# Layer 1's sort in a two-layer graph kernel: sums by even quarters, group ends looked up from two sides, tables of two values, first rows by small transfers

## The chip, the cores and the metric

One core of a Trainium2 chip runs the whole program. The metric is the device time of one execution in microseconds (us), as the median of several runs. The profile is of one further execution of the same program.

## The reference, cut to what matters

Two graph layers follow each other over 2708 nodes with 128 features and a dense 0/1 matrix `adj`. Only the second one is touched by the change:

```python
XW = X @ W                                   # X: output of layer 0
s_col, s_row = XW @ a[0, :f], XW @ a[0, f:]
Z1  = leaky_relu(s_row[:, None] + s_col[None, :], 0.01)
den = exp(Z1)
num = A @ den
att = where(num != 0, den / num, 0)
x   = layernorm(X + A @ (att @ XW))
```

`den[k, j]` depends on the sign of `s_row[k] + s_col[j]` alone in its form: it is `exp(s_row) * exp(s_col)` on one side and the same with 0.01 in the exponents on the other. So the kernel orders the nodes k by `-s_row` and the nodes j by `s_col`, cuts both orders at common thresholds into 24 groups of at most 126 nodes, and keeps running sums: for the nodes j of one group only the 126 rows k of the same group need a mixed treatment, all others are in two sums, carried from group to group in rows 0 and 1 of a 128-row operand.

## The kernel before, in words

**Layer 0** ends with a pass (L696) over six strips of 512 columns of the transposed matrix (`strip0` to `strip5`, the last 148 wide); each strip gives 4 blocks of nodes (the last one 2) their layer 0 output `x1`, and with it `s_row`, `s_col` (tiles `sr_p`, `sc_p`), `x1 @ W` (`xw`, sent to memory) and counts of nodes beyond 256 thresholds (`tally`, into `cnt`). `e2_w` holds `exp(0.01 s_row)` per node, 32 columns wide, as weights.

**Sums over everything** (`tot`, PSUM, two banks) are the start of the carried rows: `e2_w` of each of 22 row blocks times the whole row block of the transposed matrix. Each product uses 32 of TensorE's columns (`tile_position=(0, 32 * q)`), so that products with different q stand side by side. A job `total_early(kb)` ("e") loads columns 0 to 1535 of row block kb into one of three `nat` buffers, by a transfer that POOL issues, and takes them in four pieces of 384 columns, q = 0 to 3. A job `total_kept(kb)` ("k") takes strips 3, 4 and 5, which are still in SBUF, with 512, 512 and 148 columns, q = 0 to 2. Five "e" each are done at strips 3 and 4; the other 12 and all 22 "k" are strewn as fillers (`fill("kekkek...")`) among TensorE's instructions of the sort.

**The sort** starts when `strict` is set at the last strip: from there `pinned` (L163 to L167) ties every instruction of TensorE, VectorE and part of ScalarE's to the one before, so that the order in the program is the order on the engine. That is why nearly all its lines are L167. POOL and SP follow the scheduler's own order. Its steps are:

1. The counts go to all partitions (`ct`, `spread_ps`), and `reached` finds for each of 256 thresholds how far one group starting there can go (`nxt_b`, L654, L780).
2. `ends` (L827 to L834): 23 dependent look-ups in `nxt_b`, one for each group after the first, then `hit`, `thr_ps`, `thr`: the 24 thresholds in use.
3. For k, then j: `beyond` (`k_gt`), `grouped_by` (`k_hot`: node in group; `k_run`: its number there; `ahead`), `placed` (`k_onp`: node at place, in two halves), `valued` (L898: 22 small ScalarE products for each value, `k_ons`), `table` (`tab_ps`, 22 products of 32 columns per value, then `sel`). k has three values, node number, `exp(s_row)` and `exp(0.01 s_row)`; j has two, node number and `s_col`.
4. `gather` (L954): an indirect transfer, issued by POOL, of a group's 126 rows of the transposed matrix into `ring` (4 buffers over the memory of the strips); `gather_xw` (L964) the same of `xw` into `xws`.
5. `carry_in` (L987): `tot` is copied (`carried`), turned to rows 0 and 1 of `ring[0]` by 7 TensorE products (`in_ps`) and 7 copies.
6. The weights of groups 0 to 3: `c_s`, `g_s`, products `gb`, then `weights` (L1050) on ScalarE. Those of groups 4 to 23 go through memory (`g_d`, then a spread to all partitions, L1072).

**The main loop** (L1128) has 24 steps of `num` (6 products), a logarithm, a subtraction, an exponential and, three steps later, 5 products into `m_acc`. **The last part** multiplies once more by the matrix, read again from memory (L1228), and normalizes. Some checks on sizes (L1182 to L1207) feed a branch at the end; the scheduler put several of them into the sort.

Of the kernel before, what the change touches and what calls it, by code (L numbers as in the profile page):

```python
# [15 lines left out]
P = 128  # L16
# [20 lines left out]
PARTS = ((0, 1024), (1024, 2048), (2048, TAIL), (TAIL, N))  # L37
KEPT = 3
# [6 lines left out]
def grouped(  # L45
# [64 lines left out]
    def counted(name, pattern, base, step, size):  # L110
# [23 lines left out]
    row0, row1, rest, head = (  # L134
        const.tile([P, 1], F32, name=n) for n in ("row0", "row1", "rest", "head")
# [4 lines left out]
    def constants():  # L140
        dve("tensor_scalar", pad, node, N - 0.5, 1e6, ALU.is_gt, ALU.mult)
        dve("tensor_scalar", from_n, node, float(-N), None, ALU.add)
        dve("tensor_scalar", after_node, node[:, 0:2], 1.0, None, ALU.add)
        dve("tensor_scalar", row0, node[:, 0:1], 0.0, None, ALU.is_equal)
        dve("tensor_scalar", row1, node[:, 0:1], 1.0, None, ALU.is_equal)
        dve("tensor_scalar", rest, node[:, 0:1], 1.5, None, ALU.is_gt)

        dve("tensor_scalar", head, node[:, 0:1], 1.5, TINY, ALU.is_lt, ALU.max)
        dve("tensor_reduce", four, ident.rearrange("p (q g) -> p g q", q=4), AX.X, ALU.add)
# [33 lines left out]
    def act(op, *args, **kwargs):  # L183
        if strict:
            pinned("ACT", getattr(nc.scalar, op), *args, **kwargs)
        else:
            getattr(nc.scalar, op)(*args, **kwargs)  # L187

# [421 lines left out]

    tot = ps_tot.tile([P, 2, SW], F32, name="tot")
    early = KEPT * SW // 4

    def total_early(kb):
        a = nat.tile([P, KEPT * SW], F32, tag="nat", name="nat")
        nc.gpsimd.dma_start(a, adj_t[ts(kb, P), : KEPT * SW])
        for q in range(4):
            mm(
                nc.tensor.matmul, tot[32 * q : 32 * q + 32, 0, :early], e2_w[:, kb, :],
                a[:, q * early : (q + 1) * early],  # L620
                start=(kb == 0), stop=(kb == NB - 1),
                tile_position=(0, 32 * q), skip_group_check=True,
            )

    def total_kept(kb):
        for q in range(NS - KEPT):
            s = KEPT + q
            mm(
                nc.tensor.matmul, tot[32 * q : 32 * q + 32, 1, : width(s)], e2_w[:, kb, :],
                strips[s][:, kb, : width(s)],  # L630
                start=(kb == 0), stop=(kb == NB - 1),
                tile_position=(0, 32 * q), skip_group_check=True,
            )

# [8 lines left out]

    kept = [(total_kept, kb) for kb in range(NB)]
    others = [(total_early, kb) for kb in range(10, NB)]

    def fill(pattern):

        for c in pattern:
            f, kb = (kept if c == "k" else others).pop(0)  # L650
            f(kb)


    nxt_b = late.tile([P, Q], F32, name="nxt_b")  # L654
# [11 lines left out]
    def reached(ct_ps):  # L666

        nxt = small.tile([P, 2], F32, tag="nxt", name="nxt")
        for h in range(2):
            more = work2.tile([P, SW], F32, tag="junk", name="more")[:, :Q]  # L670
            dve("tensor_scalar", more, ct_ps[:, :Q], ct[:, h : h + 1], None, ALU.subtract)
            dve(
                "scalar_tensor_tensor", more, ct_ps[:, Q:], ct[:, 2 + h : 3 + h], more,
                ALU.subtract, ALU.max,
            )
            fits = work2.tile([P, SW], F32, tag="junk", name="fits")[:, :Q]
            dve(
                "tensor_scalar", fits, more, G + 0.5, 0.0, ALU.is_lt, ALU.add,
                accum_out=nxt[:, h : h + 1],
            )  # L680
        return nxt
# [14 lines left out]
    for s in range(NS):  # L696
# [32 lines left out]
        if strict:  # L729
            fill("ekkk")  # L730
# [6 lines left out]
        )  # L737

# [10 lines left out]
        if strict:  # L749

            dve("tensor_reduce", ct, cnt.rearrange("p s k h -> p (k h) s"), AX.X, ALU.add)
            fill("k")
            ct_ps = spread_out(ct, 4)
            fill("k")
# [11 lines left out]
        nc.scalar.activation(e2_p[:, mine], low[:, mine], AF.Exp, scale=LEAK)  # L766
        nc.gpsimd.tensor_copy(e2_w[:, mine, 1], e2_p[:, mine])
        if strict:
            nxt = reached(ct_ps)
            nxt_ps = spread_out(nxt, 2)  # L770
        pn = ps_mm.tile([P, SW // P, D], F32, tag="mm", name="xw_ps")
# [5 lines left out]
        xw = work2.tile([P, SW // P, D], F32, tag="xw", name="xw")  # L777
        if strict:
            nc.scalar.copy(xw[:, :nb, :], pn[:, :nb, :])
            dve("tensor_copy", nxt_b, nxt_ps[:, :Q])  # L780
# [6 lines left out]
        if s in (3, 4):  # L787
            for kb in range(5 * s - 15, 5 * s - 10):
                total_early(kb)
    fill("kekkekkekkekkk")  # L790
# [20 lines left out]
    e1_p = tab.tile([P, NB], F32, name="e1_p")  # L811
    nc.scalar.activation(e1_p, low, AF.Exp)
# [8 lines left out]
    ons = {"k": (3, None), "j": (2, None)}  # L821
    for name, (m, _) in ons.items():
        t = tmp.tile([P, m, NB, 32], F32, name=name + "_ons")
# [3 lines left out]
    ends = tmp.tile([P, NG], F32, name="ends")  # L827
    dve("tensor_copy", ends[:, 0:1], nxt_b[:, 0:1])
    for g in range(1, NG):
        junk = tmp.tile([P, Q], F32, tag="more", name="junk")  # L830
        dve(
            "scalar_tensor_tensor", junk, bound_no, ends[:, g - 1 : g], nxt_b,
            ALU.is_equal, ALU.mult, accum_out=ends[:, g : g + 1],
        )  # L834
    thr_ps = ps_x.tile([P, SW], F32, tag="x", name="thr_ps", bufs=2)
    for h in range(2):
        hit = tmp.tile([P, NG], F32, tag=f"hit{h}", name="hit")
        dve(
            "tensor_scalar", hit, ends, after_node[:, h : h + 1], theta[:, h : h + 1],
            ALU.is_equal, ALU.mult,  # L840
        )
        mm(
            nc.tensor.matmul, thr_ps[:, :NG], ones, hit, start=(h == 0), stop=(h == 1)
        )
    fill("kkk")
    thr = tmp.tile([P, NG + 1], F32, name="thr")
    nc.gpsimd.memset(thr[:, 0:1], -1e9)
    dve("tensor_copy", thr[:, 1:], thr_ps[:, :NG])


    def beyond(name, v):

        gt = tmp.tile([P, NG + 1, NB], F32, name=name + "_gt")
# [3 lines left out]
    def grouped_by(name, gt):  # L857
# [3 lines left out]
        run = tmp.tile([P, NG, NB], F32, name=name + "_run")  # L861
# [9 lines left out]
        return hot, run, ahead, of  # L871

    def placed(name, hot, run, ahead):

        dve(
            "tensor_tensor", ons[name][:, 0, :, :NG].rearrange("p b g -> p g b"), hot,
            along(from_n, NG, NB), ALU.mult,
        )
        dve("tensor_tensor", run, run, over(ahead[:, :NG], NG, NB), ALU.add)
        own = tmp.tile([P, NB, NG], F32, tag="own", name=name + "_own")  # L880
        dve("tensor_tensor", own.rearrange("p b g -> p g b"), run, hot, ALU.mult)
        at = tmp.tile([P, NB], F32, name=name + "_at")
        dve("tensor_reduce", at, own, AX.X, ALU.add)

        halves = []
        for b0, b1 in ((0, 12), (12, NB)):
            onp = tmp.tile([P, b1 - b0, P], F32, tag=f"onp{b0}", name=f"{name}_onp{b0}")
            dve(
                "tensor_tensor", onp, over(at[:, b0:b1], b1 - b0, P),
                along(col, b1 - b0, P), ALU.is_equal,  # L890
            )
            halves += [onp[:, b, :] for b in range(b1 - b0)]
        return halves

    def valued(name, k, hot, val):

        for b in range(NB):
            nc.scalar.activation(  # L898
                ons[name][:, k, b, :NG], hot[:, :, b], AF.Identity, scale=val[:, b : b + 1]
            )  # L900

    def table(name, onp, values, ps, p0=0, between=""):

        t = tmp.tile([P, len(values), P], F32, name=f"{name}_t{values[0]}")
        for b0 in range(0, NB, 4):
# [8 lines left out]
        for n, o in enumerate(ps):  # L914
            nc.scalar.copy(t[:, n, :], o)
        if callable(between):
            between()
        else:
            fill(between)
# [17 lines left out]

    k_gt = beyond("k", vk)
    k_hot, k_run, k_ahead, k_of = grouped_by("k", k_gt)
    valued("k", 1, k_hot, e1_p)  # L940
    valued("k", 2, k_hot, e2_p)
    fill("ekkekkee")
    j_gt = beyond("j", vj)
    k_onp = placed("k", k_hot, k_run, k_ahead)
    k_tab, _ = table("k", k_onp, [0], banks("x"), P - G)
    j_hot, j_run, j_ahead, j_of = grouped_by("j", j_gt)
    k_no = rows_of_table("k", k_tab, G)
    valued("j", 1, j_hot, sc_p)
    k_tab, _ = table("k", k_onp, [1, 2], banks("x", "ahead"), between="eee")
    assert not kept and not others, (len(kept), len(others))  # L950

# [21 lines left out]
    j_onp = placed("j", j_hot, j_run, j_ahead)  # L973
    carried = tmp.tile([P, 2, SW], F32, name="carried")
    nc.gpsimd.memset(carried, 0.0)
    for r0, r1, k, c in ((0, P, 0, early), (0, 64, 1, SW), (64, 96, 1, width(NS - 1))):
        nc.scalar.copy(carried[r0:r1, k, :c], tot[r0:r1, k, :c])
# [5 lines left out]
    carried_parts = [(q, 0, q * early, early) for q in range(4)] + [  # L983
        (s - KEPT, 1, s * SW, width(s)) for s in range(KEPT, NS)
    ]

    def carry_in(*nos, by, ps=None):  # L987

        for n in nos:
            q, k, i0, c = carried_parts[n]  # L990
            o = (ps or ps_x).tile(
                [P, SW], F32, tag="num" if ps else "sel", name="in_ps", bufs=3 if ps else 2
            )
            mm(
                nc.tensor.matmul, o[:2, :c], ident[:, 32 * q : 32 * q + 2],
# [700 lines left out]
```

## Time and profile before

| | us |
|---|---|
| median of 3 runs (762.22 to 765.44) | 762.48 |
| the profiled execution's own time | 763.92 |
| its span, first to last instruction | 762.0 |
| last strip's first step in the sort (`h`) | 359.2 |
| first look-up of `ends` | 373.06 |
| first `num` of the main loop | 419.12 |
| `num` of steps 8 to 23, start to start | 8.84 |
| first `h_acc` of the last part | 649.33 |

Times in the trace are from the start of the span. A row of the timeline gives start, duration, engine, line, operation, result and operands, how often, and in brackets how long the engine stood idle before it and what ended that. TensorE takes each float32 product in two passes, so x8 in a row is four products. A row of merged instructions spans gaps, and PE rows of the four column groups lie over each other. The table of stretches gives for each engine its busy time and instructions, then the share of the TensorE clock that was granted, the busy share of the DMA engines and their rate.

### The profile page before, as it was taken

What the parts mean: (1) busy time and instruction counts of PE and PEld (TensorE: products, weight loads), DVE (VectorE), ACT (ScalarE), POOL (GpSimd) and SP (SyncE); (2) the same over time, 40 slices, a digit from 0 to 9 for tenths busy, and PEclk for the clock granted to TensorE, in tenths of its full rate; (3) what the DMA queues carried; (4) which work ended last, traced back from release to release, by engine and by line L of the source; (5) the groups of instructions that cost most, each with busy time, mean ns of one, the idle gap of its engine ahead of it and who ended that gap; (6) DMA issues with size and microseconds to landing.
All of it is one profiled execution on the core that took longest, in us unless ns stands there. A gap on an engine that the chain in (4) does not pass through costs nothing. (4 is left out here: it accounts for less than half of the span.)

```text
span 762.0 us, 7796 instructions
## 1 busy us (share of the span) xinstructions
PE 721.7 (95%) x2561; PEld 350.4 (46%) x2561; DVE 453.2 (59%) x947; ACT 419.7 (55%) x601; POOL 259.1 (34%) x255
## 2 busy tenths in 40 slices
PE   6989999999997999999898799999999999999995
PEld 4434454545553444445334344444444445544444
DVE  4786776664631443235895998998999982203032
ACT  4747777868551222112264599999999994001000
POOL 6857696979741000001124887111111000000000
PEclk9999999999998999999999999999999999999999
DMA  8738988898989996535369835964444430898970
GB/s 299 282 134 317 313 321 310 321 342 302 345 305 412 379 346 240 188 125 208 117 243 241 255 102 187 223 187 158 173 171 143 157 135 1 269 314 301 319 236 22
DMA packets 67522, 179.87 MB, mean 236 GB/s; under 512 B 4238, under 2 KB 18354, under 8 KB 64450
## 3 DMA queue, kind: packets, MB, share of 16 engines
q1 hardware_dynamic: 52996, 123.10, 45.7%
q0 software_dynamic: 8208, 53.30, 22.1%
q10 hardware_dynamic: 6270, 2.90, 1.3%
q8 instruction: 22, 0.36, 0.2%
q14 instruction: 26, 0.21, 0.1%
HBM read 176.44 MB, written 2.84 MB: 235 GB/s over the span
## 5 line engine op out<-in xcount | busy, mean ns | idle before, releaser
L541 POOL TENSOR_TENSOR total<-total,p_t 128x512 f32<-128x512 f32 (+2 forms) x132 | 152.4, 1155 | 44.5 <-ACT p_t L187 28.3
L167 PE MATMUL num<-ring,wt 128*128 128x512 f32 (+1 forms) x288 | 128.3, 545 | 7.5 <-DVE q L167 4.9
L167 PE MATMUL m_acc<-q,xws 128*128 128x512 f32 x240 | 120.5, 592 | 0.4 <-ACT q L167 0.4
L703 PE MATMUL dif_acc<-strip,x_sb 128*128 128x512 f32 (+1 forms) x264 | 107.7, 557 | 5.3 <-DVE x_sb L582 4.6
L181 DVE SCALAR_TENSOR_TENSOR p_t<-sim,gentle,piece 128x512 f32<-128x512 f32 (+1 forms) x111 | 71.3, 670 | 50.2 <-PE sim L175 35.9
L175 PE MATMUL att_acc<-p_t,x_sb 128*128 128x512 f32 (+1 forms) x228 | 97.2, 545 | 3.4 <-ACT p_t L187 3.1
L167 DVE COPY q<-num 128x512 f32<-128x512 f32 x144 | 86.4, 613 | 16.6 <-PE num L167 15.5
L1233 PE MATMUL h_acc<-ring,m_sb 128*128 128x512 f32 x220 | 95.7, 593 | 0.0
L187 ACT ACTIVATE p_t<-p_t,shift 128x512 f32<-128x512 f32 (+1 forms) x111 | 69.4, 656 | 31.4 <-DVE p_t L181 30.8
L167 PEld LDWEIGHTS num<-ring,wt 128*128 128x128 f32 x288 | 51.5, 190 | 67.4 <-issue 55.7
L167 DVE SCALAR_TENSOR_TENSOR q<-sr_b,nc_s,q 128x1536 f32<-128x1536 f32 (+1 forms) x48 | 77.4, 1613 | 1.2 <-ACT q L167 1.2
L167 ACT ACTIVATE q<-q,head,rest 128x1536 f32<-128x1536 f32 (+1 forms) x48 | 70.5, 1509 | 8.5 <-DVE ring L167 4.5
L703 PEld LDWEIGHTS dif_acc<-strip,x_sb 128*128 128x128 f32 x264 | 47.2, 194 | 56.0 <-issue 49.5
L167 PEld LDWEIGHTS m_acc<-q,xws 128*128 128x128 f32 x240 | 45.5, 190 | 57.1 <-issue 55.7
L954 POOL DMA_INDIRECT ring<-in_adj_t,k_no x24 | 33.5, 1397 | 108.0 <-PE num L167 103.1
L167 ACT ACTIVATE row<-row 128x1354 f32<-128x1354 f32 x44 | 58.3, 1324 | 17.6 <-DMA row<-in_adj 17.2
L1233 PEld LDWEIGHTS h_acc<-ring,m_sb 128*128 128x128 f32 x220 | 41.3, 190 | 49.3 <-issue 49.3
L167 ACT ACT_TABLE_LOAD x48 | 61.6, 1283 | 3.8 <-issue 2.9
L167 ACT ACTIVATE q<-q,c_s 128x1536 f32<-128x1536 f32 (+1 forms) x48 | 62.7, 1354 | 0.3
L175 PEld LDWEIGHTS att_acc<-p_t,x_sb 128*128 128x128 f32 x228 | 39.1, 190 | 49.6 <-ACT p_t L187 27.6
L1248 DVE TENSOR_TENSOR hh<-rows,x 128x512 f32<-128x512 f32 (+1 forms) x6 | 3.8, 641 | 85.2 <-PE rows L1171 82.5
L1243 ACT COPY ht<-h_acc 128x512 f32<-128x512 f32 (+1 forms) x6 | 3.2, 536 | 91.3 <-PE h_acc L1233 91.2
(270 smaller groups left out, 823.0 us busy)
## 6 DMA issues: line engine op xcount, KB each, us to landing
row<-in_adj SPq DMA_DIRECT2D x44, 677.0 KB, 5.8
strip<-in_adj_t SPq DMA_DIRECT2D x10, 2816.0 KB, 14.8
ring<-in_adj_t SPq DMA_DIRECT2D x27, 1024.0 KB, 5.0
piece<-in_adj_t SPq DMA_DIRECT2D x24, 1024.0 KB, 6.2
nat<-in_adj_t POOLq DMA_DIRECT2D x22, 768.0 KB
piece<-in_adj_t SPq DMA_DIRECT2D x7, 512.0 KB, 6.0
strip<-in_adj_t SPq DMA_DIRECT2D x2, 814.0 KB, 13.8
last<-in_adj_t POOLq DMA_DIRECT2D x1, 1628.0 KB
```

What stands on the lines that cost most here:

```text
L167: latest[engine] = op(*args, **kwargs)
L175: op(*args, **kwargs)
L181: getattr(nc.vector, op)(*args, **kwargs)
L187: getattr(nc.scalar, op)(*args, **kwargs)
L541: nc.gpsimd.tensor_tensor(total[:r, :v], total[:r, :v], p_t[:r, :v], ALU.add)
L703: nc.tensor.matmul(acc[:, :v], x_sb[:, jb, :], st[:, jb, :v], start=(jb == 0), stop=(jb == NB - 1),)
L954: nc.gpsimd.indirect_dma_start(out=ring[g % RING][P - G :, :], out_offset=None, in_=adj_t[:, :], in_offset=bass.IndirectOffsetOnAxis(ap=k_ ...
L1233: nc.tensor.matmul(acc[:, : h1 - h0], m_sb[:, kb + b, :], a[:, b, h0:h1], start=(kb + b == 0), stop=(kb + b == NB - 1),)
L1243: nc.scalar.copy(ht[:, h0:h1], acc[:, : h1 - h0])
L1248: nc.vector.tensor_tensor(hh[:, b0 : b0 + n, :], rows[:, :n, :], x1[:, ib + b0 : ib + b0 + n, :], ALU.add)
```

## The change

- "k" takes the kept columns in four quarters of 293, q = 0 to 3; a quarter that runs over the end of a strip is taken in two pieces, so a job has 6 products instead of 3. Strips 3 and 4 have four "e" each, so 14 stay for the sort; those are loaded by transfers that SP issues. The fill patterns are new.
- At strip 4 no exponential is taken; the last strip's one covers both (`s != NS - 2`).
- `reached` needs two VectorE instructions for each half instead of three. `ends`: partitions 0 to 63 go up from the first threshold, partitions 64 to 127 down from the last one, with 11 look-ups at once. For that the number of fitting thresholds is also summed over partitions by two products of 256 columns (`ones` by `fits`), and one more product (`ends_ps`) brings both sides together.
- k's table has two values, number and `s_row`, and j's number and a clipped `s_col`; the exponentials come after the table, of 24 columns. Node numbers of k are valued by ScalarE, those of j by VectorE. `onp` is made in one instruction.
- `carry_in` is gone: eight transfers of 2 rows, issued by SP, take `carried` to rows 0 and 1 of `ring[0]`.
- The first four groups' weights come from products of `four` by `j_t` between j's table and its `sel`; group 0's exponential and weights go first.
- The checks are tied behind the main loop. The order on POOL has all four first `gather` ahead of the first `gather_xw`; before, three.

The core of the diff:

```diff
-    others = [(total_early, kb) for kb in range(10, NB)]
+    quarters = (KEPT * SW // 4, (N - KEPT * SW) // 4)
+    def first_strips(kb, eng):
+        a = nat.tile([P, KEPT * SW], F32, tag="nat", name="nat")
+        eng.dma_start(a, adj_t[ts(kb, P), : KEPT * SW])
+        for q in range(4):
+            sum_part(0, q, kb, 0, a[:, ts(q, quarters[0])])
+    def kept_strips(kb, eng):
+        for _, q, s, i, c, n in sorted(kept_parts):
+            sum_part(1, q, kb, c, strips[s][:, kb, i : i + n])
...
-            fill("ekkk")
+            fill("kekek")
...
+            for h in range(2):
+                mm(nc.tensor.matmul, nxt_ps[:, Q:], ones, fits[h], start=(h == 0), stop=(h == 1))
...
-    fill("kekkekkekkekkk")
+    fill("kekekkekek")
...
-    for g in range(1, NG):
+    for g in range(1, half_g):
...
+    mm(nc.tensor.matmul, ends_ps[:, : NG - 1], ones, both, start=True, stop=True)
...
-    valued("k", 1, k_hot, e1_p)
-    valued("k", 2, k_hot, e2_p)
-    fill("ekkekkee")
+    valued("k", 0, k_hot, from_n)
+    valued("k", 1, k_hot, low, 0, 18)
+    fill("kekekek")
     j_gt = beyond("j", vj)
...
-    k_tab, _ = table("k", k_onp, [0], banks("x"), P - G)
+    k_tab, _ = table("k", k_onp, [0], banks("x"), P - G, between=lambda: fill("e"))
+    valued("k", 1, k_hot, low, 18)
+    j_run, j_ahead, j_of = numbered("j", j_hot)
+    fill("ke")
+    valued_by_dve("j", 0, j_hot, from_n)
     k_no = rows_of_table("k", k_tab, G)
-    valued("j", 1, j_hot, sc_p)
-    k_tab, _ = table("k", k_onp, [1, 2], banks("x", "ahead"), between="eee")
+    for n, c in enumerate(quarters):
+        act("copy", carried[:, n, :c], tot[:, n, :c])
...
+    for n, c in enumerate(quarters):
+        for q in range(4):
+            i = n * KEPT * SW + q * c
+            nc.sync.dma_start(ring[0][:2, i : i + c], carried[32 * q : 32 * q + 2, n, :c])
     for g in range(2):
         gather(g)
+    j_own = chosen("j", j_hot, j_run, j_ahead)
+    valued("j", 1, j_hot, cs_p)
+    k_tab, _ = table("k", k_onp, [1], banks("x"))
+    j_onp = placed("j", j_own)
...
+    def first_weights():
+        gb_ps = ps_x.tile([P, 4, P], F32, tag="x", name="gb_ps", bufs=2)
+        for g in range(4):
+            mm(nc.tensor.matmul, gb_ps[:, g, :], four[:, g : g + 1].to_broadcast([P, P]), j_t_of[1], ...)
+        act("activation", gb[:, 0, :], gb_ps[:, 0, P - G :], AF.Exp)
+        weights(0, gb[:, 0, :])
+        act("activation", gb[:, 1:, :], gb_ps[:, 1:, P - G :], AF.Exp)
+    j_tab, j_t = table("j", j_onp, [0, 1], banks("x", "ahead"), between=first_weights)
```

## The prediction

> **What bounds the kernel now.** I read the page's busy shares, then the table of stretches, then each engine's timeline over the sort. TensorE is busy 95% of the span, but not everywhere with work that counts:
>
> ```profile
> core 0: us, PE busy (x) PEld busy (x) DVE busy (x) ACT busy (x) POOL busy (x), PEclk, DMA share, GB/s
> ...
> 372.00:387.00 15.00, 14.99 (x110) 5.73 (x111) 13.19 (x55) 0.37 (x1) 4.00 (x8) 0.89 0.64 219
> 387.00:400.00 13.00, 11.18 (x130) 4.92 (x130) 12.72 (x18) 11.89 (x51) 2.18 (x5) 1.00 0.57 193
> 400.00:406.00 6.00, 4.30 (x112) 3.10 (x100) 5.83 (x6) 4.21 (x19) 5.39 (x3) 1.00 0.84 247
> 406.00:419.10 13.10, 11.94 (x128) 6.31 (x121) 3.85 (x14) 4.19 (x12) 3.67 (x5) 0.87 0.96 238
> ...
> 480.00:690.00 210.00, 208.88 (x569) 99.60 (x568) 144.60 (x187) 159.54 (x148) 16.70 (x15) 1.00 0.56 176
> ```
>
> In the main loop (480 to 690) TensorE is the bound. In the sort its busy time is mostly filler. What sets the sort's length changes: VectorE to 400, then TensorE's written order.
>
> ```profile
> L167 DVE SCALAR_TENSOR_TENSOR junk<-bound_no,ends,nxt_b x23: 484/485/486, 373.1 to 384.7; 128x256 f32<-128x256 f32 x23
> ```
>
> The 23 look-ups start 0.53 us apart (373.06, 373.59, 374.12): 373.06 to 385.24.
>
> ```profile
> 388.11 10.44 ACT L898 ACTIVATE k_ons<-k_hot,e_p 128x24 f32<-128x24 f32 x44 [15.02 <-DVE k_hot L167]
> ...
> 405.52 0.85 PE L167 MATMUL tot<-nat,e_w 128*32 128x384 f32 x8 [1.70 <-DMA nat<-in_adj_t]
> 406.30 0.62 PE L167 MATMUL k_sel<-four,k_t 128*128 128x24 f32 x4
> 407.02 2.08 PE L167 MATMUL in_ps<-carried,ident 128*2 128x384 f32 x3
> ...
> 409.54 3.18 PE L167 MATMUL tab_ps<-j_onp,j_ons 128*32 128x128 f32 x82
> 412.56 0.81 PE L167 MATMUL in_ps<-carried,ident 128*2 128x384 f32 x2
> ```
>
> After 402, j's table waits behind the last "e" (a late load), k's `sel` and the carry-in. `num` starts at 419.12, and everything behind it follows.
>
> **The change, step by step.** Times are before -> after in the profile's time.
>
> *Price of the fillers.* The timeline shows an "e" at 379.07 and the next at 381.43: 2.36 us for two "k" and one "e", 2 x 2 x 512 + 2 x 384 = 2816 columns of one column group, 0.838 ns each. So "k" costs 0.86 and "e" 0.64; the new "k" has 293 columns in each group, 2 x 293 x 0.838 = 0.49.
>
> *1. Strips 3 and 4.* Two "e" leave a stretch where PE is busy 50.8 of 51 us (305 to 356). One lies ahead of strip 4's `sb_ps` (354.56), whose VectorE work ends only at 359.2: -0.64.
>
> *2. Last strip.* Strip 4's exponential goes, and with it two table switches (1.28 us each); `rstd` waited for the second (VectorE idle 0.98). `xw_ps` now stands after one "k" and a quarter of an "e", so VectorE's 1.27 idle there stays nearly whole. With 0.64, 0.98 and the stray check (0.14): `x1` turned at 364.26 -> 362.5. Filler before it: 3 x 0.49 + 2 x 0.64 + `xw_ps` 1.16 from 358.0, done by 362.0: no wait.
>
> *3. Counts and `reached`.* Same lengths to `more` (368.73 -> 367.0). Six instructions and three checks took 2.96 us; four take 2 x (0.40 + 0.53) = 1.9, end 368.9. "kek" (1.62) ends at 368.6, so it does not hold the spread. New behind it: two products of 256 columns (4 x 256 x 0.838 = 0.86), then `xw_ps`, ScalarE's `xw` copy (0.37) and, queued behind that, its half of `reach_b` (0.37). Look-ups start 373.06 -> 371.75.
>
> *4. Look-ups.* 12 fewer x 0.53 = -6.36: end 385.24 -> 377.6. "kekekkekek" (5.5 us from 370.6) ends by 377.
>
> *5. New joint.* 385.24 to 386.60 was `hit`, `thr_ps`, `thr`; now two `both` (0.25), `ends_ps` (0.40, as `ahead`), `hit`, `thr_ps`, two `thr`, two `cs_p` (0.20): 2.5. `k_gt` 386.6 -> 380.1.
>
> *6. k's table.* VectorE's `k_ons` (0.95) goes: `k_onp` 394.03 -> 386.5. It is now whole before the first product: 3.05, 389.6. `tab_ps` 22 products (1.4) to 391.0. ScalarE has 22 + 18 values at 10.44 / 44 = 0.237: from 381.55 to 391.0, a tie. `k_t`, one "e" (0.64), `sel`: 398.98 -> 391.75. `k_no` (behind `j_ons` by VectorE, 1.12) 399.44 -> 392.9; `gather` 399.94 -> 393.5.
>
> *7. The last fillers.* "ke" ends at 393.7. ScalarE, in order: four values, then the two `carried` copies wait for it (to 394.8), then 22 `j_ons` (5.3, to 400.1; 403.9 before), then k's second `k_t`. Queued behind that wait are j's values and everything of ScalarE's; TensorE waits at `k_sel` to 400.4, with j's table behind it. VectorE's `j_onp` is ready at 399.1, hidden by 1.3.
>
> *8. j's table.* From 400.8, after `k_sel`. 88 passes at the row's 82 in 3.18, or k's 86 in 2.71 at full clock: 2.8 to 3.4. Here a rule speaks against the change. The row first: 406 to 419.1 had a granted clock of 0.87, 13.1 x 0.13 = 1.7 us lost, with PE busy 91%. The Trainium skill, "TensorE: Matmul & The Clock Gate" (The HAM clock gate), says that TensorE falls to half clock after an idle window of about 3.4 us and needs as long busy to return. The new order leaves it idle from 395.1 to 400.4. By the row alone the table ends at 403.9; by the rule it runs at half clock to about 404, 1.5 more. I take 1.4: 405.2.
>
> *9. To the first `num`.* 14 passes of carry-in go. `j_t` copies (0.48), four `gb` products (0.86 + 0.2), exponential 0.3, weights 0.45: 407.4, against 419.12. Not shown before: whether the exponential waits for all four products (0) or one (-0.5); I take all. That is **-11.7**.
>
> *10. Main loop.* No instruction changes, but one stall may go:
>
> ```profile
> PE num L167 <- DMA ring<-in_adj_t,k_no: 1.5, 1, 1.5
> ```
>
> It is group 6, issued by POOL at 459.91 behind 20 `gather_xw`; now it stands behind 17, and group 5 behind 8 instead of 11: **-1.5**. The first groups land about 6 us apart (227 GB/s in 408 to 418 for 1.37 MB each), the first some 8 us after its issue at 393.5: 401.5, 407.5, 413.5, 419.5, needed at 407.4, 412.6, 419.4, 427.5.
>
> *11. Queues.* SP had nothing in the sort but `g_d`; now 14 loads stand ahead of that, each waiting until the "e" three before it has freed its buffer. The nearest row, `ring` in the page's issues, has 1.02 MB in 5.0 us; an estimate from it for 0.79 MB is 4. So the load issued at 371.7 lands at 375.7, 0.7 after TensorE could take it, inside the 0.9 that "kekekkekek" has to spare, and all later ones land 1 us or more before their "e". At 6 us each the last would come 1.4 late, which is in the second rival. POOL loses 12 such issues (0.53). The four `gather` go ahead of `gather_xw`: `xws` 2 us later, first needed at 440. The tied checks stand after `m_sb`, where VectorE idles: 0; otherwise 0.9 us.
>
> *12. Eight small transfers.* Nearest row:
>
> ```profile
> 416.60 0.39 SPq L1038 DMA_DIRECT2D g_d<-g_r  x1
> 422.74 0.68 SPq L1072 DMA_DIRECT2D wt<-g_d  x1
> ```
>
> The second issue waited for the first to land: 6.1 us at most, under gathers. Issues 8 x 0.39 from 394.8 end at 398; + 6.1 = 404, 3.4 before `num`: cost 0. If they queue for one another, see the rivals.
>
> Sum -13.2: 763.92 -> 750.7. The profiled execution is 1.44 over the median 762.48, so **749.3**.
>
> **Rivals.**
>
> *Given back to transfers, about 754.* `wt` of groups 4 on: `g_d` issued near 408, landed 414, spread 14.7 us, 428.8; wanted 24.7 after `num` starts (443.8 - 419.12), at 432. The slack falls from 6.4 to 3.3, as `g_d` gains less than `num`. Four gathers instead of three run then. 8 us late costs 5: 754. The same if "e" loads need 6 us (+1.5 to 2 at step 7) and group 6 stays late. For: DMA share 0.96 in 406 to 419. Against: POOL's loads no longer share the gathers' queue.
>
> *Slower: the eight small transfers in single file.* Place: `num` of group 0 and SP's queue, with `g_d` behind. The Trainium skill ("DMA: Bandwidth & Descriptors", Why a DMA increments its semaphore by 16 and not by 1) puts a 2-row copy on two engines only, always the same lowest ones; its fixed price there (Anatomy of one DMA) is about 2 us. Eight at 2 us in file would end at 411, +3.4: 752.7. At `g_d`'s 6.1 each they end at 443.6: 786. It decides from (419.1 - 394.8) / 8 = 3.0 us each. Against: nothing in the trace shows the next waiting for the last, and `g_d`'s 24 rows took 6.1 together.
>
> *No change.* The 23 look-ups do become 11 in the instruction order, so it does what it says; only if transfers hold the loop throughout would it show nothing. The loop runs at PE 99% from 480 on, against it.
>
> **How the numbers follow.** The sum: 0.64, with 746.5 to 752 (clock -1.4, exponential -0.5; step 7 and the loop stall +1.5 each). Given back: 0.25, 752 to 758. Within 0.5% (3.8 us, about what a measurement of this kernel can tell from no change): 0.06. Slower: 0.05. Faster in all 0.89. Range 745 to 757, which leaves the last part of the second case and the last two outside.
>
> **What would show it.** Right: look-ups x11; `k_gt` near 380; `k_sel` twice, the second after ScalarE's j values; PE idle about 5 us before j's table and a clock below 1 there; first `num` 406 to 409; no wait of `num` on a ring; SP's small transfers landed before. Wrong: `num` waiting on `carried` transfers, PE's "e" waiting on `nat`, ScalarE waiting for `wt` at step 2, or `num` before 404.

## The result, and the profile after

The changed kernel takes 765.85 us (median of 20 runs); the kernel before, run beside it, 762.43 (20 runs). The ratio is 1.0039, 95% interval 1.0019 to 1.0059: slower by 0.4%, where 749.3 was forecast. The ratios leave out the few executions that took over 1.5% more than the fastest of their kernel.

The profiled execution of the changed kernel has a span of 767.8 us against 762.0. Both are cut here at the same instructions. The first row ends at POOL's third copy into `e2_w`, ahead of all that the change touches but one small constant, and differs all the same, from execution to execution: it lay between 304.2 and 309.7 in the 18 profiles of this study, so one profile can't rank two kernels here.

| us | before | after | difference |
|---|---|---|---|
| start to that copy | 306.30 | 309.69 | +3.39 |
| copy to `num` 0 | 112.82 | 103.58 | -9.24 |
| `num` 0 to `num` 8 | 66.38 | 78.27 | +11.89 |
| `num` 8 to the end of `num` 23 | 141.52 | 141.52 | 0.00 |
| the rest | 134.98 | 134.76 | -0.22 |

The sort is 9.2 shorter in this pair, and the first eight steps of the loop give back 11.9. The 9.2 is the upper end: in the three experiments below whose sort is that of the kernel before, but for POOL's order (e2, e6, e10), copy to `num` 0 took 110.7 each, so 2.1 of it may belong to the one profile before, with its wait of 1.7 for an "e" and half clock behind it. The changed sort took 103.1 to 107.9 in the profiles below that leave it alone. The 11.9 are step 6 (7.1 longer), step 7 (2.3), step 4 (1.9) and step 2 (0.6, which e10 has too).

A time after is called "moved" below when 3.39 is taken off it, so that it can be held against the prediction. The table of stretches of the changed kernel:

```profile
core 0: us, PE busy (x) PEld busy (x) DVE busy (x) ACT busy (x) POOL busy (x), PEclk, DMA share, GB/s
...
400.00:406.00 6.00, 1.13 (x14) 1.05 (x18) 3.55 (x3) 5.09 (x23) 5.12 (x3) 0.74 0.70 242
406.00:413.20 7.20, 6.17 (x98) 5.31 (x90) 0.94 (x7) 1.76 (x7) 1.47 (x2) 0.74 0.97 244
413.20:444.00 30.80, 26.63 (x60) 11.24 (x60) 28.44 (x37) 19.04 (x19) 20.76 (x13) 0.94 0.97 223
444.00:492.00 48.00, 38.33 (x89) 17.01 (x89) 32.69 (x41) 40.27 (x37) 29.11 (x19) 0.93 0.51 144
492.00:690.00 198.00, 196.99 (x535) 94.12 (x534) 138.57 (x185) 150.84 (x139) 16.75 (x15) 1.00 0.50 169
```

In 444 to 492 TensorE is idle for almost 10 us and its clock is below 1, while the DMA engines are busy 51% of the time only. So bytes are not short there; something is issued late. From TensorE's waits and its timeline:

```profile
PE num L169 <- DMA ring<-in_adj_t,k_no: 6.9, 1, 6.9
...
PE k_sel L169 <- ACT k_t L169: 5.0, 1, 5.0
PE tot L169 <- DMA nat<-in_adj_t: 4.0, 5, 1.5
...
ACT wt L169 <- DMA wt<-g_d: 3.7, 1, 3.7
PE num L169 <- ACT tails L169: 2.5, 2, 1.3
```

```profile
404.87 0.62 PE L169 MATMUL k_sel<-four,k_t 128*128 128x24 f32 x2 [4.95 <-ACT k_t L169]
405.42 4.91 PE L169 MATMUL tab_ps<-j_onp,j_ons 128*32 128x128 f32 x88
...
413.27 1.98 PE L169 MATMUL num<-ring,wt 128*128 128x512 f32 x4 [0.72 <-ACT g_r L169]
...
480.44 2.05 PE L169 MATMUL num<-ring,wt 128*128 128x512 f32 x2 [6.91 <-DMA ring<-in_adj_t,k_no]
482.28 1.91 PE L169 MATMUL m_acc<-q,xws 128*128 128x512 f32 x2
```

The 6.9 is the gather of group 7, and the two products behind it take 2 us instead of 1: the clock is at half until 484.8.

```profile
478.00:484.80 6.80, 4.36 (x5) 1.85 (x6) 0.69 (x1) 4.09 (x4) 0.59 (x1) 0.50 1.01 288
```

POOL's timeline (of the changed kernel) shows why that gather is late: it stands behind all 24 `gather_xw`, which can start only when `j_no` is there.

```profile
412.80 1.04 POOL L1008 DMA_INDIRECT xws<-xw_d,j_no  x1 [5.70 <-DVE nc_s L169]
...
422.33 1.50 POOL L1008 DMA_INDIRECT xws<-xw_d,j_no  x1 [1.42 <-DMA ring<-in_adj_t,k_no]
429.29 1.00 POOL L1008 DMA_INDIRECT xws<-xw_d,j_no  x1 [5.46 <-DMA ring<-in_adj_t,k_no]
...
456.27 1.39 POOL L998 DMA_INDIRECT ring<-in_adj_t,k_no  x1 [0.30 <-issue]
...
472.52 1.73 POOL L998 DMA_INDIRECT ring<-in_adj_t,k_no  x1 [0.30 <-PE num L169]
```

The first and the last of these rows in the kernel before:

```profile
414.72 1.04 POOL L964 DMA_INDIRECT xws<-xw_d,j_no  x1 [8.51 <-DVE j_no L167]
...
468.76 1.08 POOL L954 DMA_INDIRECT ring<-in_adj_t,k_no  x1 [0.30 <-issue]
```

From the first `gather_xw` to group 7's gather POOL needed 54.0 us before and 59.7 after. It used to arrive just in time: step 7 followed its issue by 7.9 in both kernels, without a wait before. Now TensorE wants it sooner and gets it later.

Group 6, the row at 456.27, is late as well. Step 5 takes 10.61, as it took 10.55 before with its wait of 1.5 for that gather. Step 6's `num` started at 464.45, 8.2 after the issue (7.8 before). The row of this 1.3 names ScalarE's `tails`, which `num` doesn't read, so I take the wait to be the gather's. Step 4 is 1.9 longer (8.84 to 10.69): ScalarE waited 3.7 for `wt<-g_d`.

### The profile page after: what moved, and what is told of

Its sections match the earlier page's. It is cut to its first block, busy times and chain, and to the rows that moved or that the text cites. A ratio compares the mean times of both kernels' runs of the same rounds, so it can differ in the third digit from the quotient of the medians.

```text
span 767.8 us, 7942 instructions
## 1 busy us (share of the span) xinstructions
PE 714.3 (93%) x2639; PEld 357.8 (47%) x2639; DVE 444.8 (58%) x920; ACT 415.4 (54%) x596; POOL 251.0 (33%) x240
## 5 line engine op out<-in xcount | busy, mean ns | idle before, releaser
L169 PE MATMUL num<-ring,wt 128*128 128x512 f32 (+1 forms) x288 | 131.7, 556 | 13.3 <-DMA ring<-in_adj_t,k_no 6.9
```

The source lines that it names most:

```text
L169: latest[engine] = op(*args, **kwargs)
```

## The experiments

The theory at first (1): POOL's chain sets group 7's gather, so an earlier `num` 0 can't be used. Rivals: the DMA engines are simply full (2); the late `wt` and half clock are the main part (3); the sort isn't shorter at all (4). Each ratio is to the kernel before on the same chip; steps and stretches are of one profile each.

**e1, POOL's order written out**, and **e2, the same for the kernel before.** `pinned("POOL", ...)` ties the transfers (the core of the edit):

```diff
-        nc.gpsimd.indirect_dma_start(
+        pinned("POOL", nc.gpsimd.indirect_dma_start,
...
-        gather_xw(g)
     for g in range(2, RING):
         gather(g)
+    for g in range(4):
+        gather_xw(g)
```

So POOL's order is four gathers, four `gather_xw`, then at each step one of each.

> The changed kernel with POOL's transfers in an order written out: four gathers, four gather_xw, then at each step one gather and one gather_xw. Theory 1 (group 7's gather is late because POOL starts it only behind all 24 gather_xw, counted from j_no): num no longer waits for a ring, steps 6 and 7 fall from 15.99 and 11.10 us to about 8.9, so 9 us less than the changed kernel: ratio to before about 0.991 (755 to 757 us). Rival 2 (the gathers themselves land late because the DMA engines are full with four of them): the wait only moves to another group, within 2 us of the changed kernel, ratio 1.00. Rival 3 (late wt and half clock are the main part): step 4 stays at 10.7, at most 2 us are won.

Measured: 1.0080 [1.0052, 1.0109]. Steps 5 to 8 are 8.83 each, the ring's wait is gone, and yet nothing is won: steps 3 and 4 take 14.62 and 13.86.

```profile
ACT wt L169 <- DMA wt<-g_d: 9.8, 1, 9.8
...
PE num L169 <- ACT wt L169: 5.3, 1, 5.3
```

> The kernel before with the same written order of POOL's transfers as in the first run. Theory 1: before had a wait of only 1.5 us for group 6 and its group 7 was issued 8 us early, so it gains about 1.5 us: ratio 0.998. If this order were worth the same to both kernels (the change is not what makes it matter), it gains 8 us or more: 0.99.

Measured: 1.0047 [1.0020, 1.0073], a loss as well; `num` 0 to `num` 8 is 70.2, with steps 3 and 4 at 10.63 and 12.37. So theory 1 was half right: the ring's wait was POOL's order, but with four gathers first ScalarE waited for `wt` in both kernels (9.8 and 5.8). Rival 3 lives.

**e3, POOL's order of the kernel before in the changed one.**

> The changed kernel with POOL's transfers in exactly the order of the kernel before (3 gathers, 4 gather_xw, 1 gather, 3, 1, 4, 1, 9, 1, 4, 1). Theory 1, in the form that the chain of 24 gather_xw from j_no is the limit whatever its order: group 7 is issued 54 us after j_no (412.8) at about 467 instead of 472.5, so the stall falls from 6.9 to about 1.5 to 2: ratio about 0.997. If the order had nothing to do with it (rival 2), the same as the changed kernel, 1.004.

Measured: 1.0016 [0.9995, 1.0037]. With three gathers first, steps 0 to 4 have no stall (5.26, 6.76, 8.75, 9.12, 8.83); the ring's wait is 5.1 and comes one group earlier (steps 5 and 6: 14.11, 11.53). This order too leaves group 6's gather behind 20 `gather_xw`: it was issued 45.1 after `num` 0, 40.8 in the kernel before.

**e4, no `gather_xw` at all** (`xws` by one plain load on SP, which leaves out the choice of rows by `j_no`).

> The changed kernel with xws loaded by one plain transfer on SP's queue, so that POOL has only the gathers (left out: the gather of xw by node; xws holds the rows in their own order). Theory 1: no ring wait at all, like the first run, ratio 0.991 or a little lower. Rival 2: num still waits for rings of groups 4 to 7, since the four gathers and their 1.37 MB each stay: 1.00. Rival 3: wt of group 4 stays late by 2 to 4 us; the time of this run against the first shows what POOL's xws chain costs beside the stall.

Measured: 1.0083 [1.0051, 1.0115]; no wait for a gather, but `num` waited 3.5 for the carried rows and step 0 took 9.82. The load that took the place stands on SP's queue ahead of the carried rows and `g_d`, so it says only that POOL's chain made the ring's wait.

**e5 and e6, `wt`'s load cut in two**, with e1's and e2's order:

```diff
-    nc.sync.dma_start(wt[:, 4:, P - G :], g_d[4:] ...)
+    for g0, g1 in ((4, 8), (8, NG)):
+        nc.sync.dma_start(wt[:, g0:g1, P - G :], g_d[g0:g1] ...)
```

> The first run (changed kernel, POOL's order written out) with the load of wt cut in two: groups 4 to 7 first (258 KB), then groups 8 to 23. In the first run wt's one load of 1.26 MB took 25 us beside four gathers and num of group 4 waited 5.3 us, then ran at half clock (steps 3 and 4: 14.62 and 13.86 us). Theory 1b (the first ten groups' transfers, gathers and wt together, no longer fit in the shorter time; whichever is last in the queues stalls TensorE, and the stall costs a half-clock stretch on top): no stall is left, steps 3 and 4 take 9.1 and 8.8, num 0 to num 8 66 us instead of 75.7: 10 us less than the first run, ratio to before 0.99 to 0.995. Rival 2 (the DMA engines are full, so the stall moves to a gather, ring 4 to 7): steps still sum to 72 or more, ratio 1.00 or above.

Measured: 1.0109 [1.0073, 1.0145]. Worse: the wait for `wt` grew to 12.2 (TensorE's to 7.7), though only 0.26 of the 1.29 MB were asked for first. The DMA view shows it, from the issue to about the landing, first of e1, then of e5 (queue, kind, packets, MB, share):

```profile
q0 software_dynamic: 609, 4.28, 78.8%
q1 hardware_dynamic: 272, 1.29, 23.8%
```

```profile
q0 software_dynamic: 787, 5.12, 83.9%
q1 hardware_dynamic: 1668, 0.83, 21.2%
```

In e1 `wt` came in packets of 5,040 bytes, in e5 in packets of 504 (ten weight rows or one), beside gathers whose packets have 10,832. In 25 us it got 1.29 MB the one way and 0.83 in 26 us the other. In direction that fits the Trainium skill, "DMA: Bandwidth & Descriptors" (Queues, rings and completion order): an engine takes turns between queues by whole packets, so small packets beside large ones get less. In size it doesn't: an estimate by that rule, one packet each in turn, gives `wt` 32% of the bytes in e1 and 4% in e5, and it got 23% and 14%. And of the 0.83 MB at most 0.26 were the first piece: the second, issued 0.4 behind it, went through beside it, so small packets aren't shown to be the only cause. `g_d`, 24 packets of 504 bytes, took 9.3 us from its issue to that of `wt` (413.24 to 422.57), 6.1 before; that may have the same cause.

> The second run (kernel before, POOL's order written out) with the load of wt cut in two in the same way. Theory 1b: its steps 3 and 4 (10.63 and 12.37) fall to 9.1 and 8.8, num 0 to num 8 66 us: about the kernel before or 1 us under it, ratio 0.998 to 1.0. The difference between this run and the one of the changed kernel is then the sort alone, 5 to 9 us. If the sort had not become shorter (theory 4: the change's gain in it was run noise), both would come out the same.

Measured: 0.9987 [0.9966, 1.0009], `num` 0 to `num` 8 65.1 us. As expected here; `wt` was in time for the later `num` 0. e5 is slower than e6 by its loop (76.9 against 65.1), though its sort is 7.6 shorter (copy to `num` 0, 103.1 against 110.7): rival 4 is out.

**e7, more "e" ahead of the look-ups.** `kekek, k, kk, kek, kekekkekek, kekek, kekekek` became `eekek, e, ke, eke, kekkkkkekk, kekkk, kekkkek`.

> The changed kernel with both edits and the fillers regrouped: seven of the 14 e (first strips' rows, each needing a load of 0.79 MB) stand before the look-ups instead of three, k in their place later, the number of each the same. In four profiles of the changed sort TensorE waited 2.6 to 4.4 us for these loads, and in two of the four a wait of 2.3 us in the look-ups was followed by half clock and the sort took 4.2 us longer. Theory 5 (from 380 to 393 the e ask for 0.79 MB each 1.1 us where the engines bring one in 2.3): waits for nat fall under 1 us and the last-look-up to k_sel time is 23 us or less in every run: 2 to 3 us less than the run with the split load alone on the median. Rival (the waits are hidden behind VectorE): same time.

Measured: 1.0129 [1.0090, 1.0167]. Worse again: TensorE waits only 0.6 for `nat` in the sort, but the look-ups start 1.4 later, behind the longer filler, and TensorE waits 12.1 for `wt`. **e8** added k's second table ahead of j's values and six idle products:

> As the run before, and k's second table ahead of j's values on ScalarE, with six matmuls of 128x256 that nothing reads between the second k_sel and j's table. The wait of 4.9 us at k_sel goes; TensorE waits at j's table for j_onp and the last values instead, but not idle. Clock rule (half clock after the idle stretch): j's table takes 2.7 to 3.4 instead of 4.9, and num 0 comes 2 to 4 us earlier. Rival: j's table follows ScalarE's last value, num 0 comes 0 to 1 us earlier, and what is won is given back to the gathers, which are not issued earlier.

Measured: 1.0091 [1.0065, 1.0117]. The wait at `k_sel` went, and the first 47 passes of j's table took 1.51 at full clock, but the rest followed ScalarE: from the first `k_sel` to `num` 0 15.2 instead of 16.3, and TensorE waits 13.0 for `wt`. The rival was right.

**e9 and e10: three gathers, four `gather_xw`, the fourth gather, then one of each per step**, in the changed kernel and in the one before.

> The changed kernel with POOL's order: three gathers, four gather_xw, the fourth gather (so far the order of the kernel before), then at each step one gather and one gather_xw. In the third run this beginning left steps 0 to 4 without a stall (5.26, 6.76, 8.75, 9.12, 8.83), in the first run this ending left steps 5 to 8 without one. Theory 1c (two stalls that feed on one another: group 7's gather behind 24 gather_xw, and wt's load starved while POOL keeps four gathers of 10,832-byte packets in the queues): both are gone, num 0 to num 8 65 to 66 us instead of 78.3, ratio to before 0.988 to 0.995 (the upper end if the sort has its half-clock stretch of 4 us). Rival (a full DMA stalls TensorE whatever the order): num 0 to num 8 72 us or more, ratio 1.00 and above.

> The kernel before with the same order of POOL's transfers. Theory 1c: only its own small stalls (10.55 at step 5, about 2 in all) can go, ratio 0.997 to 1.0; the distance to the run of the changed kernel with this order is what the sort itself brings, 5 to 9 us. Rival (the order alone makes the gain, not the sort): the same time as the changed kernel with it.

Measured: e9 1.0007 [0.9986, 1.0029], e10 0.9989 [0.9961, 1.0017]. e9's profile has 67.3 us for `num` 0 to `num` 8 and no wait over 1.2 at a `num`; the median doesn't follow. e10's loop has no stall (65.1, 1.3 less than before), and no gain clear of noise. **e11**, k's second table first on top of e9:

> The changed kernel with POOL's order of the two runs before this, and k's second table ahead of j's values on ScalarE with six matmuls that nothing reads ahead of j's table. In the run that had this part, the second k_sel to num 0 and the wait ahead of it took 15.2 us instead of 16.3. Theory 1c: num 0 1 us earlier than in the run without it, and since no transfer is in the way now, 1 us less in all. Rival (what the sort wins is given back to the gathers): wt or a ring is waited for again and the time is the same or longer.

Measured: 1.0031 [1.0010, 1.0053], and TensorE waits 5.9 for `wt` again (ScalarE 12.0, 3.6 in e9). That is what the rival says, but `num` 0 came only 0.5 sooner after the copy than in e9's profile, so one profile of each can't show that the sooner `num` 0 made the wait. If the wait changes that much from execution to execution, e9's good profile and its median can both be right; that isn't shown.

**e12, one "e" moved ahead** (`kk` to `ke`, `kekekkekek` to `kekkekkkek`), nothing else, and **e13**, the same with e9's order.

> The changed kernel alone, with one e moved: the second k behind the layer norm becomes an e, and the fourth e of the look-ups becomes a k, so that each load from the seventh on is issued one e earlier. Theory 5: in five profiles of the changed sort, from the end of the look-ups to the first k_sel it took 14.85 three times and 15.3 and 19.1 (twice) when a wait of over 2 us for an e was followed by half clock. With the loads in time it takes 14 us or less and no nat wait is over 0.5: 1 to 3 us less than the changed kernel on the median, ratio 1.000 to 1.003. Rival (the loads' waits are hidden behind VectorE): 14.8 as before and ratio 1.004.

> The changed kernel with that e moved and POOL's order of the ninth run (three gathers, four gather_xw, the fourth gather, then one of each per step). If the sort's waits and the loop's stalls are the whole of what was given back, it gains what the two gain by themselves: sort as in the run with the e alone, num 0 to num 8 67 us or less, ratio 0.993 to 0.998. Rival (a faster sort is given back to wt, as when k's second table went first): wt is waited for by 3 us or more, ratio 1.00.

Measured: e12 1.0053 [1.0030, 1.0075], e13 0.9998 [0.9966, 1.0031]. In e12 look-ups to first `k_sel` took 14.2 instead of 14.85, with one wait of 2.0 left; the median isn't better than the changed kernel's. Theory 5 isn't supported as a cause of the loss.

**e14, the weights' rows of groups 4 to 7 spread by TensorE**, on top of e13:

```diff
+    gb4_ps = ps_x.tile([P, 4, P], F32, tag="x", name="gb4_ps", bufs=2)
+    for g in range(4):
+        mm(nc.tensor.matmul, gb4_ps[:, g, :], four[:, g + 4 : g + 5].to_broadcast([P, P]), j_t[:, 1, :], ...)
+    act("activation", gb[:, 4:, :], gb4_ps[:, :, P - G :], AF.Exp)
-    nc.sync.dma_start(wt[:, 4:, P - G :], g_d[4:] ...)
+    nc.sync.dma_start(gw, g_d[4:] ...)
-                weights(g + 2, wt[:, g + 2, P - G :])
+                weights(g + 2, gb[:, g + 2, :] if g + 2 < 8 else gw[:, g - 2, :])
```

> As the run before, and the weights' rows of groups 4 to 7 spread by TensorE as those of groups 0 to 3 are (four more products of 128x128 and one exponential), the load from g_d going into a tile of its own in rows of 10,080 bytes, first needed for group 8. Theory 1c: no wait for wt is left in steps 2 to 6 whatever the gathers do, num 0 comes 0.5 to 1 us later, num 0 to num 8 64.5 to 66 us; ratio 0.990 to 0.996. Rival (DMA is full): num then waits for the ring of group 4 or 5 instead, same time as the run before.

Measured: **756.59 us against 762.50, 0.9921 [0.9892, 0.9951]**: faster than the kernel before and the changed one. Its steps are 5.16, 6.77, 8.71, 9.12, 8.83, 8.84, 8.83, 8.83, and TensorE in the stretch where the changed kernel lost most:

```profile
444.00:480.00 36.00, 36.00 (x91) 16.56 (x90) 33.03 (x42) 35.76 (x33) 8.74 (x8) 1.00 0.57 189
```

The edit does two things: groups 4 to 7 need no load, and the load of the others has packets of 10,080 bytes. Which of them counts isn't separated. The profile is of an execution of 752.25; the 18 lie between 751.67 and 762.11, so some still lose time that no trace here shows.

**e15**, k's second table first on top of e14:

> As the run before, and k's second table ahead of j's values on ScalarE with the six matmuls that nothing reads. With wt out of the way its 1 us at num 0 is kept: ratio 0.989 to 0.995. Rival: the first groups' gathers, which are issued no earlier, are waited for in steps 1 to 3 by as much as num 0 is earlier, and the time is that of the run before.

Measured: 0.9923 [0.9896, 0.9951], no better. `num` 0 comes 3.1 earlier after the copy of strip 2, and now the gathers, which don't, are waited for:

```profile
412.93 4.53 PE L169 MATMUL num<-ring,wt 128*128 128x512 f32 x10 [1.76 <-DMA ring<-in_adj_t,k_no]
...
432.41 2.05 PE L169 MATMUL num<-ring,wt 128*128 128x512 f32 x2 [5.18 <-DMA ring<-in_adj_t,k_no]
```

**e16, the weights by TensorE alone.**

> The changed kernel with only the part that spreads the weights' rows of groups 4 to 7 by TensorE (POOL's order and the fillers as in the changed kernel). If the two stalls are separate: wt's 3.7 goes (step 4: 8.8 instead of 10.7), the wait for group 7's gather behind 24 gather_xw stays at 6 to 8 us with half clock behind it, num 0 to num 8 about 75, ratio 1.000 to 1.003. If wt's load was the whole cause: as the fourteenth run, 65 us and 0.992.

Measured: 0.9984 [0.9958, 1.0010]; `num` 0 to `num` 8 75.8 us.

```profile
PE num L169 <- DMA ring<-in_adj_t,k_no: 9.7, 3, 7.3
```

That closes the square: neither edit 1.0039, POOL's order 0.9998 to 1.0007 (with and without the moved "e"), `wt`'s rows 0.9984, both 0.9921 (with the moved "e", which alone gained nothing). The two stalls are separate, and with either of them left no gain is clear of noise. With both gone it is: e14 and e10 have the same loop of 65.1 us, e14's sort is 7.6 shorter (103.1 against 110.7), and their ratios are 0.0068 apart, 5.2 us. Rival 2 is out as the bound: e14 moves the same gathers and `num` waits for none.

## Why the prediction was wrong

The sort went as worked out, with sizes off; the loop went against it. The steps are those of the prediction.

- *Steps 1 and 2* (strips, last strip): -0.64 didn't come: the last strip's `h` starts at 359.4 moved, 359.2 before. The last "e" of strip 4 waited 1.35 for its load. From `h` on step 2 held: `x1` is turned 3.9 later, as forecast. The look-ups started at 372.7 moved, not 371.75.
- *Step 4* (12 look-ups fewer) was exact: 12.14 to 5.78. The group of the changed kernel:

```profile
L169 DVE SCALAR_TENSOR_TENSOR junk<-bound_no,ends,reach_b 128x256 f32<-128x256 f32 x11 | 5.3, 485 | 0.4
```

- *Step 5* (joint): 2.4, forecast 2.5. *Step 6* (k's table): first `k_sel` 393.3 moved instead of 391.75, behind two "e" that waited 1.5 and 0.4 for their loads. *Step 11* had all loads land 1 us early, from 4 us each; in 384 to 388 the DMA engines were full at 410 GB/s, and "ke" asks for 0.79 MB each 1.1 us. TensorE waited 4.0 in all.
- *Step 7* (the wait of `k_sel`) held: 4.95 idle, second `k_sel` at 401.5 moved, forecast 400.4.
- *Step 8* (j's table): 4.91, forecast 4.4 with the clock's 1.4 in it. The rule of the clock gate was right against the row: the granted clock fell to half when TensorE had stood idle 3.0 us (399.9 to 402.9), and stayed there for nearly the whole table (405.4 to 410.3):

```profile
402.90:409.70 6.80, 4.83 (x84) 4.46 (x86) 1.23 (x5) 2.19 (x11) 3.59 (x3) 0.50 0.89 294
```

- *Step 9*: `num` 0 at 409.9 moved, forecast 407.4: -9.2 for -11.7.
- *Step 10 failed*: "No instruction changes, but one stall may go: -1.5". It came to +11.9. The step counted places in POOL's queue and not when the queue starts. The `gather_xw` start with `j_no`, which moved by 5.3 (414.72 to 409.4 moved) when `num` 0 moved by 9.2, so all behind them stood 3.9 later against `num` 0. For group 6 the three places brought 1.7 of that back (43.5 from the first `gather_xw` to its gather, 45.2 before), and its stall stayed. And the step stopped ahead of group 7, which stands behind 24 `gather_xw` in both kernels: 5.7 more on POOL (59.7 for 54.0) and the 3.9 put its gather 9.6 later against `num` 0. *Step 11* then put the four gathers ahead at "`xws` 2 us later, first needed at 440": true of `xws`, but who waited was the transfer behind them, and two `gather_xw` stood still 6.9.
- *Step 12* (eight small transfers): no cost, as taken; `num` 0 waited for ScalarE's `g_r`. SP issued them 0.6 apart, not 0.39. The slower rival, single file, was wrong; its 2 us is the cited page's figure for transfers that GpSimd issues, and these are SP's.
- *Given back to transfers, 754* named `wt` and its cause, that `g_d` gains less than `num` 0. In size `wt` itself was over: 5 us were put down for it, and step 4 lost 1.9, though `g_d` to `wt` took 9.3, not 6, and the spread from there 19.4, not 14.7. Group 6 staying late, which this rival has too, came true. The larger part is in no term of it: group 7's gather, and the half clock behind that stall (step 7: 2.3 more).
- *No change*, that transfers hold the loop throughout, came nearest in time, but not in cause: from step 8 on a step takes 8.84 as before.

What isn't settled: how often the changed kernel's own executions wait for `wt` and for "e", since each profile is of one of them; and e9's median, which is put down to `wt` because e14 differs from e13 in the weights' rows and their load alone.

## What to carry to other kernels

When work ahead of a pipeline gets shorter, list every transfer up to the steady state with its issue, its place in the queue and what the queue's first item waits for: the gain can't be more than that of the transfer that moves least and has no slack. A queue that was just in time before is the next bound, and a stall can cost its length and a stretch of half clock behind it (6.9 and 2.3 here). A load of small rows with a deadline can come late beside gathers of long rows; here four more TensorE products of 128x128 took the place of its first part.

## What the runs showed of the hardware

- `gather_xw` waited for gathers that it doesn't use: 1.42 and 5.46 at 422.33 and 429.29 in the changed kernel. In the program such a transfer waits for the one eight places ahead of it, by eight semaphores used in turn; here these were the third and the fourth gather.
- One broadcast load cut by groups went from packets of 5,040 to 504 bytes, and its first 0.26 MB took 26 us (e5), as long as all 1.29 MB in one piece (25, e1).
- TensorE needn't be idle for the whole of the 3.4 us of which the rule cited at step 8 speaks. In e3 the clock fell to half at 381.3 after a wait of 2.3, with TensorE busy 1.68 of the last 3.41 us; in the kernel before it fell at 372.8 after 1.82 of 3.41. In e3 k's first `sel` came 19.1 after the look-ups, 4.2 later than in the changed kernel's profile:

```profile
372.00:381.30 9.30, 6.98 (x112) 4.87 (x110) 6.61 (x30) 0.75 (x2) 0.80 (x4) 1.00 0.88 299
381.30:388.10 6.80, 6.40 (x57) 4.22 (x56) 4.51 (x11) 3.29 (x14) 0.00 (x0) 0.50 0.74 258
```
